# Moving 4 of 400 embedding gathers from GpSimd to single-row fetches that SyncE issues from registers

## The chip, the cores and the metric

The kernel runs on one core of one Trainium2 chip. The metric is the device time of one execution in microseconds. The kernel before ran 17 times: median 1652.48 us, from 1648.65 to 1654.3 us.

## The reference

The inputs are 1024 sequences of 50 item numbers, a length for each, a table of 100001 embedding rows of 128 floats, and a scale and a shift. Cut to what matters:

```python
emb = emb_table.at[0].set(0.0)
e = emb[seq]                                   # 1024 x 50 x 128
prefix = jnp.cumsum(e, axis=1)
denom = jnp.minimum(t_idx[None, :], lengths[:, None])
uF = prefix / denom[:, :, None]
mean, var = uF.mean(axis=0), uF.var(axis=0)    # over the 1024 sequences
y = (uF - mean) * lax.rsqrt(var + BN_EPS) * gamma + beta
def step(v, x):                                # 50 steps, one after the other
    v = v + (x - v) / TAU
    spike = atan_spike(v - V_TH)               # 1 where v >= 1
    v = v - spike * V_TH
    return v, spike
_, spikes = lax.scan(step, v0, x_seq)
scores = spikes.mean(axis=0) @ emb.T           # 1024 x 100001
```

## The kernel before

There are two stages. The first computes, for 1024 sequences and 128 features, how many of the 50 steps spiked. The second multiplies these counts with the whole table and writes 409.6 MB of scores.

The order of the instructions on each engine is the order in which the code is written (a manual schedule); waits between engines are semaphores that the framework adds.

In the first stage a step `t` goes like this. `gather(t)` (defined at L183) asks GpSimd for eight indirect DMAs (L187), one for each block of 128 sequences: each fetches 128 table rows of 512 bytes into one 128x128 piece of the tile `e`. The tile pool `gather` has two such tiles, so the gather of step t+1 may only begin when TensorE has read the tile of step t-1. At step t the kernel first issues `gather(t + 1)`, then TensorE transposes the eight pieces of `e` into the two PSUM banks `pre[0]` and `pre[1]`, where they add to the running sum (L296, four pieces for each bank, each matmul waiting for the landing of its own piece). VectorE then scales each bank and takes its statistics (L305, L306), TensorE adds the correction for the zero row of the next step (`correct`, L253), VectorE and ScalarE form mean, variance and the normalised input (L316 to L339), VectorE updates the membrane potential `v` (L348, L342), and TensorE adds the spikes to `sums` (`counted`, L264). Steps 42 and 44 also transpose one 1024-row part of the table each, for the second stage (`prepare`).

SyncE (SP) issues, in this order: the item numbers `idx` (1024 x 50, laid out 128 partitions x 8 blocks x 50 steps), the lengths, row 0 of the table, scale and shift, then six loads of 3 MB of the table (`fetch`, L97) for the second stage, and after that nothing until the first store of scores (L158) at the stage's end. DMAs from SP use eight completion semaphores in turn, and a DMA waits until the one eight places before it has landed.

The second stage turns the table (`prepare`: L119, L141, L142), multiplies it (L149), evicts with VectorE and ScalarE (L454, L456) and stores from SP (L158).

Of the kernel before, what the change touches and what calls it, by code (L numbers as in the profile page):

```python
# [12 lines left out]
F32 = mybir.dt.float32  # L13
# [7 lines left out]
P = 128  # L21
# [4 lines left out]
BANK = 512  # L26
# [8 lines left out]
def rec_kernel(  # L35
# [9 lines left out]
    nc = tc.nc  # L45
    B, T = seq.shape
    N, D = table.shape
    NB = B // P
# [24 lines left out]
    rows = {}  # L73
# [9 lines left out]
    def group(g):  # L83
        at = g if g < AHEAD else AHEAD - 2 + g % 2
        r = rowp.tile([P, GROUP, HALF], F32, tag=f"rows{at}", name=f"rows_{g}")
        for k in range(GROUP):
            rows[g * GROUP + k] = r[:, k, :]
        return r

    def fetch(r, q, n):  # L90

        engine = nc.sync if q < AHEAD * GROUP else nc.scalar
        k = q % GROUP
        n = min(n, parts - q)
        whole = n - (size(q + n - 1) < HALF)
        if whole:
            engine.dma_start(  # L97
                out=r[:, k : k + whole, :],
                in_=table[q * HALF : (q + whole) * HALF, :].rearrange("(q p k) d -> p q (k d)", p=P, k=KQ),
            )  # L100
        if whole < n:
            full, rest = divmod(size(parts - 1), P)
            c1 = (parts - 1) * HALF
            r = r[:, k + whole, :].rearrange("p (k d) -> p k d", d=D)
            if full:
                engine.dma_start(
                    out=r[:, :full, :],
                    in_=table[c1 : c1 + full * P, :].rearrange("(k p) d -> p k d", p=P),
                )
            if rest:  # L110
                engine.dma_start(out=r[:rest, full, :], in_=table[c1 + full * P : N, :])
# [21 lines left out]
    def prepare(q, pt):  # L133
        turned(q, pt)
        split[q] = hi, lo = free.pop(0)
        hw = size(q)
        if hw % 2:
            nc.vector.memset(hi[:, hw : hw + 1].bitcast(F32), 0.0)
            nc.vector.memset(lo[:, hw : hw + 1].bitcast(F32), 0.0)
        vp, vh, vl = views(q, pt, hi, lo)  # L140
        nc.scalar.copy(vh, vp)  # L141
        nc.vector.tensor_tensor(vl, vp, vh.bitcast(F32), ALU.subtract)  # L142
# [18 lines left out]
    with ExitStack() as ph:  # L161
        once = ph.enter_context(tc.tile_pool(name="once", bufs=1))
# [7 lines left out]
        idx = once.tile([P, NB, T], I32, tag="idx", name="idx")  # L170
# [8 lines left out]
        for g in range(AHEAD):  # L179
            fetch(group(g), g * GROUP, GROUP)  # L180

        es = {}

        def gather(t):
            es[t] = gp.tile([P, B], F32, tag="e", name=f"e_{t}")
            for n in range(NB):
                nc.gpsimd.indirect_dma_start(  # L187
                    out=es[t][:, n * P : (n + 1) * P],
                    out_offset=None,
                    in_=table,  # L190
                    in_offset=bass.IndirectOffsetOnAxis(ap=idx[:, n, t : t + 1].bitcast(U32), axis=0),
                )

        make_identity(nc, ident)
        gather(0)


# [47 lines left out]
        def only(t):  # L245

            l = sp.tile([P, D], F32R, tag="l", name=f"l_{t}")
            nc.scalar.activation(l, r0n, AF.Copy, scale=sel[:, t : t + 1])
            return l

        def correct(t, l):
            for h in range(B // BANK):
                nc.tensor.matmul(  # L253
                    pre[h],
                    lhsT=l,
                    rhs=zT[:, h * BANK : (h + 1) * BANK],
                    start=t == 0,
                    stop=False,
                    skip_group_check=True,
                )  # L260

        def counted(t, s):
            for h in range(B // BANK):
                nc.tensor.matmul(  # L264
                    sums[h],
                    lhsT=ident_h,
                    rhs=s[:, h * BANK : (h + 1) * BANK],
                    start=t == 0,
                    stop=t == T - 2,
                    skip_group_check=True,  # L270
                )
# [11 lines left out]
        for t in range(T):  # L283
            last = t == T - 1
            if t + 1 < T:
                gather(t + 1)
            e = es.pop(t)
            if last:
                s = lp.tile([P, B], BF16, tag="s", name=f"s_{t - 1}")
                nc.vector.tensor_single_scalar(s, v, V_TH, ALU.is_ge)  # L290
                nc.vector.tensor_tensor(negv, s, v, ALU.subtract)
            uF = up.tile([P, B], F32, tag="uF", name=f"uF_{t}")
            bs = sp.tile([P, B // BANK, 6], F32, tag="bs", name=f"bs_{t}")
            for h, cs in enumerate(halves):
                for k in range(0, BANK, P):
                    nc.tensor.matmul(  # L296
                        pre[h][:, k : k + P],
                        lhsT=e[:, h * BANK + k : h * BANK + k + P],
                        rhs=ident,
                        start=False,  # L300
                        stop=last,
                        is_transpose=True,
                        skip_group_check=True,
                    )
                nc.vector.scalar_tensor_tensor(uF[:, cs], rlen[:, cs], 1.0 / (t + 1), pre[h], ALU.max, ALU.mult)  # L305
                nc.vector.bn_stats(bs[:, h, :], uF[:, cs])  # L306
            if not last:
                correct(t + 1, l)
            else:

                counted(t - 1, s)
                count = once.tile([P, B], F32, tag="zT", name="count")
                for h, cs in enumerate(halves):
                    nc.scalar.copy(count[:, cs], sums[h])
            mv = sp.tile([P, 2], F32, tag="mv", name=f"mv_{t}")
            nc.vector.bn_aggr(mv, bs.rearrange("p h s -> p (h s)"))  # L316


            r = sp.tile([P, 1], F32, tag="r", name=f"r_{t}")
            nc.scalar.activation(r, mv[:, 1:2], AF.Sqrt, bias=eps)  # L320
            nc.scalar.activation(uF, uF, AF.Identity, bias=mv[:, 0:1], scale=-1.0)


            if t and not last:
                s = lp.tile([P, B], BF16, tag="s", name=f"s_{t - 1}")
                nc.vector.tensor_single_scalar(s, v, V_TH, ALU.is_ge)  # L326
                counted(t - 1, s)

            nc.vector.reciprocal(r, r)
            q = sp.tile([P, 1], F32, tag="q", name=f"q_{t}")  # L330
            nc.vector.tensor_mul(q, r, r)
            nc.vector.scalar_tensor_tensor(q, mv[:, 1:2], BN_EPS, q, ALU.add, ALU.mult)  # L332
            nc.vector.tensor_scalar(q, q, -0.5, 1.5, ALU.mult, ALU.add)
            a = sp.tile([P, 1], F32, tag="a", name=f"a_{t}")
            nc.vector.tensor_scalar(a, q, r, hgb[:, 0:1], ALU.mult, ALU.mult)  # L335


            def x(vt, cs):
                nc.scalar.activation(vt, uF[:, cs], AF.Identity, bias=hgb[:, 1:2], scale=a)  # L339

            def step(vt, cs):
                nc.vector.scalar_tensor_tensor(vt, negv[:, cs], -0.5, vt, ALU.mult, ALU.add)  # L342

            if not last:
                vt = vp.tile([P, B], F32, tag=f"v{t % 2}", name=f"v_{t}")
                x(vt, whole)
                if t:
                    nc.vector.tensor_tensor(negv, s, v, ALU.subtract)  # L348
                step(vt, whole)
                v = vt  # L350
                if t + 2 < T:
                    l = only(t + 2)

                if t in (T - 8, T - 6):
                    q = (t - T + 8) // 2
                    prepare(q, vp.tile([P, HALF], F32, tag="v1", name=f"pt_{q}"))
# [53 lines left out]
    for c, W in enumerate(WIDTHS):  # L410
# [30 lines left out]
        for n in range(NB):  # L441
            if c == 0 and n == 0:
                continue
            pool, tag, most = turns[blocks % len(turns)]
# [51 lines left out]
```

## Time and profile before

| what | value |
|---|---|
| median of 17 runs | 1652.48 us (1648.65 to 1654.3) |
| the profiled execution, its own time | 1653.87 us |
| its span in the profile | 1652.1 us |
| first store of scores issued | 587.68 us after the span's start |
| GpSimd busy | 379.2 us, 23% of the span, nearly all of it in the first stage |
| VectorE busy | 939.9 us, 57% |
| TensorE busy | 1112.6 us, 67% |
| mean granted TensorE clock | 0.802 |

The profile page gives, for one execution, the busy time of each engine, the span in 40 slices, the DMA queues, the chain of work that ended last, and groups of equal instructions with busy time, mean duration and the idle time before them. The trace behind it gives the instructions in order of time (the timeline: start, duration, engine, line, operation, tile written<-tiles read, and in brackets the idle time before and what ended it), the waits of an engine, and the busy time of chosen stretches. "SPq" is an instruction that SP executes to issue a DMA; its duration is that of the issue, not of the transfer. "Remote" stands where the profile couldn't name what ended a wait.

In 40 slices of 41.3 us, GpSimd's busy share (tenths), the DMA share and the moved GB/s show the two stages; the first ends in the fifteenth slice:

```
POOL 6666666666666500000000000000000000000000
DMA  9511111111111169999999999999999999999998
GB/s 340 214 44 48 48 43 48 48 48 43 47 48 46 39 280 409 417 422 397 426 429 427 426 429 430 418 425 428 420 428 409 413 428 425 414 427 410 396 422 359
```

### The profile page before, as it was taken

How to read it: one execution, taken by the hardware profiler on the slowest of the kernel's cores; microseconds unless marked ns; L12 is line 12 of the kernel's file. 1: busy time of each engine (PE TensorE's matmuls, PEld its weight loads, DVE VectorE, ACT ScalarE, POOL GpSimd, SP SyncE). 2: the span in 40 equal slices, each digit the busy share in tenths (PEclk: the TensorE clock that was granted, in tenths of full speed). 3: DMA queues.
4: the chain of work that ended last, by engine and by line, in shares of the span. 5: the costliest groups of instructions: out<-in, count | busy, mean ns of one | idle time of the engine just before them, and what ended most of it. 6: DMA issues, size and time to landing. Idle time of an engine off the chain costs nothing.

```text
span 1652.1 us, 12555 instructions
## 1 busy us (share of the span) xinstructions
PE 1112.6 (67%) x4538; PEld 828.6 (50%) x4548; DVE 939.9 (57%) x1161; ACT 630.6 (38%) x700; POOL 379.2 (23%) x406
## 2 busy tenths in 40 slices
PE   4333334433443488889987888878888888788785
PEld 2122212211222266667766666666666666666664
DVE  4566656655665666557655455545455555555553
ACT  2222222222222255545544444444444444444442
POOL 6666666666666500000000000000000000000000
PEclk7555555555555589999999999999999999999998
DMA  9511111111111169999999999999999999999998
GB/s 340 214 44 48 48 43 48 48 48 43 47 48 46 39 280 409 417 422 397 426 429 427 426 429 430 418 425 428 420 428 409 413 428 425 414 427 410 396 422 359
DMA packets 53691, 488.14 MB, mean 295 GB/s; under 512 B 11995, under 2 KB 12796, under 8 KB 32380
## 3 DMA queue, kind: packets, MB, share of 16 engines
q1 hardware_dynamic: 31984, 428.77, 61.7%
q0 software_dynamic: 12800, 26.24, 6.1%
q10 hardware_dynamic: 8844, 32.33, 5.0%
q8 instruction: 36, 0.59, 0.1%
q14 instruction: 27, 0.22, 0.0%
HBM read 77.69 MB, written 409.60 MB: 295 GB/s over the span
## 4 chain that ended last, share of the span: by engine, by line
DMA 48%; DVE 21%; PE 10%; another core or an unknown queue 9%; ACT 6%; issue 5%; POOL 1%; DVEq 0%; ACTq 0%; SPq 0%
DMA scores<-o 47%; PE po L149 9%; ACT o L456 4%; DVE bs L306 4%; DVE uF L305 4%; DVE v L342 3%; DVE s L326 3%; DVE negv L348 2%; DVE o L454 2%; ACT v L339 1%; POOL e L187 1%; DVE a L335 1%; DVE mv L316 1%; DVE q L332 0%
## 5 line engine op out<-in xcount | busy, mean ns | idle before, releaser
L454 DVE TENSOR_SCALAR o<-po 128x1024 f32<-128x1024 f32 x391 | 463.7, 1221 | 353.0 <-DMA scores<-o 322.2
L456 ACT ACTIVATE o<-po 128x1024 f32<-128x1024 f32 (+1 forms) x391 | 388.1, 1019 | 550.2 <-DMA scores<-o 346.0
L187 POOL DMA_INDIRECT e<-in_L_rec_emb_table,idx x400 | 378.5, 946 | 187.3 <-issue 114.6
L149 PE MATMUL po<-pairs,countB 128*128 128x512 f32 x1168 | 314.7, 416 | 66.7 <-ACT o L456 49.5
L149 PEld LDWEIGHTS po<-pairs,countB 128*128 128x128 f32 x1168 | 225.9, 198 | 131.4 <-ACT o L456 64.3
L149 PE MATMUL po<-pairs,countC 128*128 128x512 f32 x876 | 238.6, 418 | 44.7 <-ACT o L456 44.7
L253 PE MATMUL pre<-zT,l 128*128 128x512 f32 x100 | 74.1, 743 | 254.6 <-DVE uF L305 188.3
L149 PEld LDWEIGHTS po<-pairs,countC 128*128 128x128 f32 x876 | 169.3, 200 | 91.0 <-ACT o L456 56.2
L253 PEld LDWEIGHTS pre<-zT,l 128*128 128x128 f32 x100 | 27.5, 277 | 294.1 <-issue 201.4
L305 DVE SCALAR_TENSOR_TENSOR uF<-rlen,pre 128x512 f32<-128x512 f32 x100 | 67.9, 679 | 175.1 <-remote 115.7
L320 ACT ACTIVATE r<-mv,eps 128x1 f32<-128x1 f32 x50 | 14.7, 295 | 373.1 <-DVE mv L316 259.2
L142 DVE TENSOR_TENSOR pairs<-pt,pairs 128x1024 fp32r<-128x1024 f32 (+1 forms) x73 | 88.4, 1217 | 96.4 <-ACT pairs L141 96.2
L296 PE MATMUL pre<-ident,e 128*128 128x128 f32 x400 | 105.4, 423 | 25.2 <-DMA e<-in_L_rec_emb_table,idx 19.0
L119 PE MATMUL pt<-ident,rows 128*128 128x128 f32 x782 | 111.3, 289 | 8.2 <-ACT o L456 3.6
L119 PEld LDWEIGHTS pt<-ident,rows 128*128 128x128 f32 x782 | 100.8, 152 | 28.6 <-issue 10.0
L296 PEld LDWEIGHTS pre<-ident,e 128*128 128x128 f32 x400 | 85.3, 223 | 58.6 <-DMA e<-in_L_rec_emb_table,idx 33.2
L149 PE MATMUL po<-hi,countB 128*128 128x512 f32 x200 | 83.5, 417 | 18.5 <-ACT o L456 14.1
L264 PE MATMUL sums<-s,ident_h 128*128 128x512 bf16 x88 | 44.9, 601 | 64.5 <-issue 34.3
L149 PE MATMUL po<-lo,countB 128*128 128x512 f32 x200 | 81.1, 405 | 0.0
L149 PE MATMUL po<-pairs,countA 128*128 128x512 f32 (+1 forms) x292 | 73.6, 394 | 10.2 <-ACT o L456 10.1
L141 ACT CAST pairs<-pt 128x1024 fp32r<-128x1024 f32 (+1 forms) x73 | 73.6, 1008 | 14.8 <-PE pt L119 14.5
L149 PE MATMUL po<-hi,countC 128*128 128x512 f32 x150 | 62.8, 419 | 16.2 <-ACT o L456 16.1
(76 smaller groups left out, 849.7 us busy)
## 6 DMA issues: line engine op xcount, KB each, us to landing
scores<-o SPq DMA_DIRECT2D x96, 3072.0 KB, 20.6
scores<-o SPq DMA_DIRECT2D x32, 1536.0 KB, 9.0
rows<-in_L_rec_emb_table ACTq DMA_DIRECT2D x20, 1536.0 KB, 30.1
scores<-o SPq DMA_DIRECT2D x22, 1024.0 KB, 8.6
rows<-in_L_rec_emb_table SPq DMA_DIRECT2D x6, 3072.0 KB, 42.7
scores<-o SPq DMA_DIRECT2D x8, 2048.0 KB, 13.2
scores<-o SPq DMA_DIRECT2D x8, 1872.5 KB, 11.3
e<-in_L_rec_emb_table,idx POOLq DMA_INDIRECT x400
```

Of the source, the lines that this page charges most:

```text
L119: nc.tensor.transpose(pt[:, k0 : k0 + kw], r[:kw, k0 : k0 + D], ident[:kw, :kw])
L141: nc.scalar.copy(vh, vp)
L142: nc.vector.tensor_tensor(vl, vp, vh.bitcast(F32), ALU.subtract)
L149: nc.tensor.matmul(po[:, :kw], lhsT=counts[n], rhs=part[:, k0 : k0 + kw], start=j == 0, stop=j == 1,)
L187: nc.gpsimd.indirect_dma_start(out=es[t][:, n * P : (n + 1) * P], out_offset=None, in_=table, in_offset=bass.IndirectOffsetOnAxis(ap=idx[: ...
L253: nc.tensor.matmul(pre[h], lhsT=l, rhs=zT[:, h * BANK : (h + 1) * BANK], start=t == 0, stop=False, skip_group_check=True,)
L296: nc.tensor.matmul(pre[h][:, k : k + P], lhsT=e[:, h * BANK + k : h * BANK + k + P], rhs=ident, start=False, stop=last, is_transpose=True, ...
L305: nc.vector.scalar_tensor_tensor(uF[:, cs], rlen[:, cs], 1.0 / (t + 1), pre[h], ALU.max, ALU.mult)
L306: nc.vector.bn_stats(bs[:, h, :], uF[:, cs])
L326: nc.vector.tensor_single_scalar(s, v, V_TH, ALU.is_ge)
L454: nc.vector.tensor_scalar_mul(o[:, h0 : h0 + hw], po[:, :hw], 1.0 / T)
L456: nc.scalar.mul(o[:, h0 : h0 + hw], po[:, :hw], 1.0 / T)
```

## The change

For the first block of 128 sequences, at the steps 44, 45, 46 and 47, GpSimd no longer gathers. In its place SP, after its six loads of the table, goes through the 128 partitions: it reads four item numbers of one partition from `idx` into registers (one instruction), and for each of the four computes the row's address in registers (one instruction for two multiplications) and issues a DMA of this one 512-byte row into a tile `aside_44` to `aside_47`. These tiles have memory of their own and are written once. That makes 128 register loads, 512 register computations and 512 DMAs on SP, all between its sixth load of the table and its first store. GpSimd issues 396 gathers, seven at each of the four steps. TensorE's first transpose of each of these steps reads `aside` in place of the first piece of `e`, and waits for the semaphores of these row fetches.

The built order shows the following besides: the fetched rows take their turn among SP's eight completion semaphores, so the eighth row fetch waits until the sixth load of the table has landed, and each later one until the row fetch eight places before has landed. The rows are fetched partition by partition, with the four steps inside, so the last row of `aside_44` is the 509th of the 512. On the other engines the order of the work is as before.

```diff
         for g in range(AHEAD):
             fetch(group(g), g * GROUP, GROUP)
 
+        aside = {}
+        for t0, many in ((T - 6, 4),):
+            for t in range(t0, t0 + many):
+                aside[t] = once.tile([P, P], F32, tag=f"aside{t}", name=f"aside_{t}")
+            for p in range(P):
+                _, items = nc.values_load_multi_w_load_instructions(
+                    idx[p : p + 1, 0, t0 : t0 + many],
+                    engines=[mybir.EngineType.SP],
+                    min_val=0,
+                    max_val=N - 1,
+                    skip_runtime_bounds_check_because="items are rows of the table; the transfer checks its own bounds",
+                )
+                for j, item in enumerate(items):
+                    nc.sync.dma_start(out=aside[t0 + j][p : p + 1, :], in_=table[bass.ds(item, 1), :])
+
         es = {}
 
         def gather(t):
             es[t] = gp.tile([P, B], F32, tag="e", name=f"e_{t}")
-            for n in range(NB):
+            for n in range(t in aside, NB):
                 nc.gpsimd.indirect_dma_start(
...
                     nc.tensor.matmul(
                         pre[h][:, k : k + P],
-                        lhsT=e[:, h * BANK + k : h * BANK + k + P],
+                        lhsT=aside[t] if h == k == 0 and t in aside else e[:, h * BANK + k : h * BANK + k + P],
                         rhs=ident,
```

## The prediction

> **What bounds the kernel now.** I read the chain of waits first, to see which stage pays for what.
>
> ```profile
> DMA scores<-o 47%; PE po L149 9%; ACT o L456 4%; DVE bs L306 4%; DVE uF L305 4%; DVE v L342 3%; DVE s L326 3%; DVE negv L348 2%; DVE o L454 2%; ACT v L339 1%; POOL e L187 1%; DVE a L335 1%; DVE mv L316 1%; DVE q L332 0%
> ```
>
> Nearly half of the chain is stores of scores, from the first at 587.68 us on. That stage is as long as its stores and isn't touched: what ends the first stage d us earlier ends the kernel d us earlier. So only the first 588 us matter. There the chain names VectorE, but the groups and GpSimd's own waits tell who paces it:
>
> ```profile
> L187 POOL DMA_INDIRECT e<-in_L_rec_emb_table,idx x400 | 378.5, 946 | 187.3 <-issue 114.6
> ```
> ```profile
> POOL e L187 <- issue: 114.6, 376, 0.3
> POOL e L187 <- remote: 63.8, 15, 5.6
> ```
>
> A gather is busy for 0.946 us and 376 of the 400 start 0.30 us after the one before: 1.25 us each, 400 x 1.25 = 500 us of the stage. The 15 waits ended by "remote" are all the slack that GpSimd has, 63.8 us. The timeline shows one, and the stage's end:
>
> ```profile
> 475.25 0.95 POOL L187 DMA_INDIRECT e<-in_L_rec_emb_table,idx  x1 [0.31 <-issue]
> 480.48 0.95 POOL L187 DMA_INDIRECT e<-in_L_rec_emb_table,idx  x1 [4.28 <-remote]
> 481.73 0.95 POOL L187 DMA_INDIRECT e<-in_L_rec_emb_table,idx  x1 [0.30 <-issue]
> ```
> ```profile
> 566.21 0.95 POOL L187 DMA_INDIRECT e<-in_L_rec_emb_table,idx  x1 [0.31 <-issue]
> 568.52 0.69 DVE L305 SCALAR_TENSOR_TENSOR uF<-rlen,pre 128x512 f32<-128x512 f32 x1 [9.54 <-remote]
> ...
> 571.40 0.69 DVE L305 SCALAR_TENSOR_TENSOR uF<-rlen,pre 128x512 f32<-128x512 f32 x1 [1.47 <-remote]
> ```
>
> Two things are to be seen. GpSimd restarts after such waits at 310.43, 344.43, 378.42, 412.44, 446.49, 480.48: every 34.0 us, 24 gathers (three steps, 30.0 us) and 4.0 us of idling for a free tile. And VectorE runs two steps 7.49 us apart (L305 at 543.91 and 551.40), then waits, and is released 5.2 us after the last gather that GpSimd could issue (566.21 to 571.40; likewise 475.25 to 480.24). Why TensorE's transposes come out so late in every third step the trace doesn't say; that their end is tied to GpSimd's last gather it does. So the stage goes at GpSimd's pace: a gather less is 1.25 us less, and VectorE has room, since its step of 7.49 us is under the 10.0 us of eight gathers or the 8.75 us of seven.
>
> **What is removed.** 4 gathers x 1.25 us = 5.0 us. They fall behind the waits of the stage, not into them, if the pattern of waits stays: step 44's missing gather releases the wait that ends at 514.75 by 1.25 us, those of 45 and 46 the one at 537.45 by 3.75 us in all, that of 47 brings the last gather from 566.21 to 561.2 us. Four transposes read another tile: the same instruction and form. Each waits for two semaphores more than before, one extra wait on TensorE, at most the 0.3 us between two of its rows here, and in steps where its data are long there: 0 taken, up to 1.2 us in the range.
>
> **What is added.** SP was idle then:
>
> ```profile
> SPq L158 <- ACT o L390: 552.2, 3, 550.5
> ```
>
> 550.5 us of waiting between the last load and the first store hide the new work as long as it ends in time. When can it start, and when must it end? The eighth row waits for the sixth load of the table:
>
> ```profile
> 40.00:60.00 20.00, 5.61 (x13) 3.28 (x15) 10.04 (x19) 2.96 (x5) 11.06 (x13) 0.50 1.03 393
> 60.00:80.00 20.00, 7.26 (x22) 4.39 (x21) 11.28 (x22) 5.63 (x8) 14.91 (x16) 0.50 0.25 69
> ```
>
> The last column is GB/s. From 80 to 100 us it is 43; the 26 above that are 0.52 MB, at 393 GB/s 1.3 us: the loads end at about 61.3 us. The first use is step 44's first transpose:
>
> ```profile
> 521.33 1.91 PE L296 MATMUL pre<-ident,e 128*128 128x128 f32 x8
> ```
>
> 521.33, less the 1.25 us gained by then: 520.1. All but 3 of the rows must have landed, so SP has 458.8 us, 0.896 us for a row or 3.58 us for a group of four. A row costs an issue, a register computation, and a quarter of a register load. Issues of other transfers:
>
> ```profile
> 2.82 0.43 SPq L177 DMA_DIRECT2D gb<-in_L_rec_gamma  x1
> 3.29 0.43 SPq L178 DMA_DIRECT2D gb<-in_L_rec_beta  x1
> 3.77 33.35 SPq L97 DMA_DIRECT2D rows<-in_L_rec_emb_table  x6
> ```
> ```profile
> 1507.25 0.35 ACTq L97 DMA_DIRECT2D rows<-in_L_rec_emb_table  x1
> 1507.63 1.28 ACTq L106 DMA_DIRECT2D rows<-in_L_rec_emb_table  x1
> 1508.94 1.72 ACTq L111 DMA_DIRECT2D rows<-in_L_rec_emb_table  x1
> ```
>
> The smallest transfers on SP (0.5 KB, like a row) follow each other by 0.47 us. The dearest issue that isn't a load of megabytes is L111, 33 partitions of 512 bytes: 1.72 us. It stands directly behind another slow one, and it is ACT's; a row has the bytes of `gb` and SP's queue. I take 0.47 and keep 1.72 as the upper end. A computation in registers has no row; the gaps between SP's issues are 0.04 to 0.05 us: 0.05 taken, 0 to 0.3 (the gap on GpSimd) possible. A load from SBUF into a register has none either: from 0 up to 3.0 us, the time in which the smallest timed DMA (`len_i`, 4 KB) goes out and lands, which is a longer way. I take 1.0 us, an estimate nearer the lower end because no DMA is in it. A group: 4 x (0.47 + 0.05) + 1.0 = 3.08 us; 128 of them 394 us; done at 455 us, 65 us before they are needed: 0 on the path. From both sides: 4 x 0.47 = 1.88 us a group, done at 302 us; or 4 x (1.72 + 0.3) + 3.0 = 11.1 us, done at 1480 us, 960 us late.
>
> The waits between row fetches cost nothing at that pace: eight rows back is 6.2 us ago, twice the landing of `len_i`. On the DMA engines the rows are 0.26 MB beside the 47 GB/s that this stretch moves: 0, or bounded in the rivals by what a delayed gather does. SP's stores come after, 130 us later: 0.
>
> The Trainium skill ("DMA: Bandwidth & Descriptors", section "Latency and other measured facts") puts the floor of a register load from a tensor at about 600 ns. By it a group would be 2.68 us and the rows done at 404 us; no row here shows one. The same page (section "Why a DMA increments its semaphore by 16 and not by 1") speaks against the change: a transfer whose shape doesn't split over 16 engines makes the issuing sequencer write the rest of the count itself. L111's 33 partitions, at 1.72 us, agree with that; if every row were such a one, a group would be 4 x 1.77 + 1.0 = 8.08 us and the rows done at 1096 us. The page gives no price for these writes.
>
> **The sum** against the profiled execution: 1653.87 - 5.0 = 1648.9; that one lies 1.39 us over the median, so 1647.5 us by the median.
>
> **The rivals.**
> - *SP is late (slower).* A row needs more than 0.896 us, which is where a load costs over 1.50 us at an issue of 0.47. TensorE waits at step 44, GpSimd stops two tiles on, and every us late is one on the end, since the steps and gathers behind it still have to be done. With a load of 2.0 us a group is 4.08 us, done at 583.5, 63.4 us late: 1647.5 + 63.4 = 1711 us. It is slower than before from 0.906 us a row. For it: L106 and L111, and that nothing here shows a load. Against: the issues at 0.47.
> - *More of the three-step waits (slower).* The rows' transfers and semaphore counts share the DMA engines with the gathers. Where a wait came after two steps instead of three (from 218.96 to 242.46) 2 steps took 23.5 us, 11.75 a step against 11.33. If that were so for the 35 steps from 62 to 455 us: 35 x 0.42 = +14.6, -5.0: 1662 us. Against: the DMA share is 0.18 there.
> - *One wait less (faster by more).* At step 48 TensorE starts its transposes at 556.31, and the last piece, issued at 556.20, makes it wait until 558.85. After the change TensorE comes 3.75 us earlier and that gather 5.0, so this wait is gone, and with it perhaps the one of VectorE up to 571.40. Then VectorE's second half of step 48 is at 552.72 - 3.75 + 7.49 = 556.5 in place of 571.4, and the last step, whose pieces land by about 564, no longer waits: -14.9, 1637.6 us. Against: step 45 shows such a wait where TensorE had not waited for a piece.
> - *Nothing.* The 5.0 us go into GpSimd's idling, a wait that something else ends: 1652.5 us. Against: the releases follow the last gather.
>
> **How the numbers follow.** The forecast has 0.44, SP late 0.22, more waits 0.08, one wait less 0.15, nothing 0.11. 0.2% is 3.3 us, about what runs of this kernel can tell from no change. The forecast is faster but for 0.03 that belong to "same": faster 0.41 + 0.15 = 0.56, same 0.11 + 0.03 = 0.14, slower 0.30. The time is the forecast's, 1647.5; its own range is 1645 to 1650. The range for 8 in 10 goes down to 1636 for the missing wait, up past 1662 to 1668, which takes in rows late by up to 20 us (0.04 of the 0.22): 0.18 left out above.
>
> **What would show it.** Right: 396 gathers 1.25 us apart, the last at about 561 us, the first store at 582.7; SP's row fetches ended before 520 us; TensorE's transposes of `aside` waiting for nothing. Each price is then read off: the spacing of row fetches within a group and between groups. Wrong: TensorE idle until a row fetch lands; more than 15 waits of GpSimd by "remote", or fewer; SP's first store held up by rows still going out.

## The result and the profile after

The changed kernel takes 1779.97 us (median of 9 runs, 1774.19 to 1785.16), the one before 1652.76 us in the runs beside it: ratio 1.0771 [1.0760, 1.0781], slower by 127 us. The profiled execution took 1787.07 us, with a span of 1785.3 us against 1652.1 before, 133.2 us more. All lines below the added code have moved by 17: the gathers are L204 now, the row fetches L197, the transposes L313, `uF` L322.

The chain of waits shows a line that was not there before, and the stores' share fell only because the whole grew:

```profile
DMA scores<-o 43%; PE po L149 8%; SPq L197 4%; ACT o L473 4%; SPq L189 2%; DVE o L471 2%; DVE bs L323 0%; DVE uF L322 0%; DVE v L359 0%; ACT pairs L141 0%; DVE s L343 0%; PE pt L119 0%; DVE pairs L142 0%; DVE negv L365 0%
```

SP's row fetches (L197) and the register loads before them (L189) stand on the path now. The groups of the page and GpSimd's own waits (engine, tile and line, what it waited for: us in total, times, the longest) say who paid:

```profile
L204 POOL DMA_INDIRECT e<-in_L_rec_emb_table,idx x396 | 374.7, 946 | 330.7 <-PE pre L313 140.6
L313 PE MATMUL pre<-ident,aside 128*128 128x128 f32 x4 | 1.7, 427 | 136.9 <-DMA aside<-in_L_rec_emb_table 136.7
```
```profile
POOL e L204 <- PE pre L313: 140.6, 3, 137.3
POOL e L204 <- issue: 111.3, 365, 0.3
POOL e L204 <- remote: 61.7, 20, 4.7
POOL e L204 <- PE pre L270: 13.4, 4, 3.5
```

Four gathers are gone at 0.946 us each, with no change in the price of the others. Against that stand two single waits: TensorE's first transpose of `aside` waits 136.7 us, and GpSimd, two tiles ahead, 137.3 us for that transpose. The timelines of TensorE and of GpSimd show them:

```profile
525.63 1.01 PE L281 MATMUL sums<-s,ident_h 128*128 128x512 bf16 x2 [1.26 <-DVE s L343]
663.36 0.45 PE L313 MATMUL pre<-ident,aside 128*128 128x128 f32 x1 [136.71 <-DMA aside<-in_L_rec_emb_table]
```
```profile
527.35 0.94 POOL L204 DMA_INDIRECT e<-in_L_rec_emb_table,idx  x1 [0.30 <-issue]
665.57 0.94 POOL L204 DMA_INDIRECT e<-in_L_rec_emb_table,idx  x1 [137.28 <-PE pre L313]
```

Step 44's transposes begin at 663.36 in place of 521.33, 142.0 us late. The first store follows 58.0 us behind them and not 66.4, since the pieces of steps 44 and 45 were there already. So it goes out at 721.37 in place of 587.68, 133.7 us late; the span grew by 133.2. All of the loss is this one wait.

SP's own timeline, cut at three windows (start, us, how many row fetches they cover):

```profile
61.98 457.90 SPq L197 DMA_DIRECT2D aside<-in_L_rec_emb_table  x264
```
```profile
539.82 120.20 SPq L197 DMA_DIRECT2D aside<-in_L_rec_emb_table  x207
```
```profile
721.37 3.62 SPq L158 DMA_DIRECT2D scores<-o  x4
```

From 62 to 520 us, while GpSimd gathers, a row takes 457.90 / 264 = 1.73 us. From 540 us on, with GpSimd and TensorE stopped for want of these rows, the same instructions take 120.20 / 207 = 0.58 us a row. The instructions of L197 by kind (in ns the shortest, the median and the longest, then the first and the last start) tell what became longer:

```profile
L197 SPq FUSED_REGOPS  x512: 2/37/1419, 37.7 to 663.2; - x171
L197 SPq MOVE aside<-in_L_rec_emb_table x512: 2/29/1398, 37.8 to 663.3; - x171
L197 SPq DMA_DIRECT2D aside<-in_L_rec_emb_table x512: 2/225/7557, 38.1 to 663.3; - x171
```

Not only the DMAs: a computation in registers, 0.037 us in the median, and a move of a register, 0.029 us, last up to 1.4 us. (The one DMA of 7.56 us is set aside here: the run with quick rows below, `f1_after`, has such a one too, 8.36 us.) What stretches such an instruction is the question of the experiments.

### The profile page after: what moved, and what is told of

Same layout as the page of the kernel before. It is cut to its first block, busy times and chain, and to the rows that moved or that the text cites. A ratio compares the mean times of both kernels' runs of the same rounds, so it can differ in the third digit from the quotient of the medians.

```text
span 1785.3 us, 14221 instructions
## 1 busy us (share of the span) xinstructions
PE 1109.4 (62%) x4538; PEld 832.3 (47%) x4548; DVE 940.5 (53%) x1161; ACT 630.9 (35%) x700; POOL 375.4 (21%) x402
## 4 chain that ended last, share of the span: by engine, by line
DMA 43%; PE 8%; SPq 6%; ACT 5%; DVE 4%; issue 4%; another core or an unknown queue 0%; DVEq 0%; ACTq 0%
DMA scores<-o 43%; PE po L149 8%; SPq L197 4%; ACT o L473 4%; SPq L189 2%; DVE o L471 2%; DVE bs L323 0%; DVE uF L322 0%; DVE v L359 0%; ACT pairs L141 0%; DVE s L343 0%; PE pt L119 0%; DVE pairs L142 0%; DVE negv L365 0%
## 5 line engine op out<-in xcount | busy, mean ns | idle before, releaser
L204 POOL DMA_INDIRECT e<-in_L_rec_emb_table,idx x396 | 374.7, 946 | 330.7 <-PE pre L313 140.6
L270 PE MATMUL pre<-zT,l 128*128 128x512 f32 x100 | 75.8, 760 | 270.4 <-DVE uF L322 216.9
L322 DVE SCALAR_TENSOR_TENSOR uF<-rlen,pre 128x512 f32<-128x512 f32 x100 | 68.1, 681 | 316.6 <-remote 161.2
L270 PEld LDWEIGHTS pre<-zT,l 128*128 128x128 f32 x100 | 28.1, 282 | 311.7 <-issue 197.3
L313 PE MATMUL pre<-ident,e 128*128 128x128 f32 x396 | 98.5, 420 | 11.9 <-DMA e<-in_L_rec_emb_table,idx 5.6
L313 PEld LDWEIGHTS pre<-ident,e 128*128 128x128 f32 x396 | 85.2, 226 | 36.2 <-issue 27.4
L313 PE MATMUL pre<-ident,aside 128*128 128x128 f32 x4 | 1.7, 427 | 136.9 <-DMA aside<-in_L_rec_emb_table 136.7
```

What stands on the lines that cost most here:

```text
L204: nc.gpsimd.indirect_dma_start(out=es[t][:, n * P : (n + 1) * P], out_offset=None, in_=table, in_offset=bass.IndirectOffsetOnAxis(ap=idx[: ...
L270: nc.tensor.matmul(pre[h], lhsT=l, rhs=zT[:, h * BANK : (h + 1) * BANK], start=t == 0, stop=False, skip_group_check=True,)
L313: nc.tensor.matmul(pre[h][:, k : k + P], lhsT=aside[t] if h == k == 0 and t in aside else e[:, h * BANK + k : h * BANK + k + P], rhs=ident ...
```

## The experiments

The runs fell on chips of two kinds. On kind A the kernel before takes 1652.2 to 1653.8 us, as in the result; on kind B 1576.2 to 1577.0 us. Each run is compared with the kernel before on its own chip. The stores' stage is alike on both: from the first store to the end of the span 1652.1 - 587.68 = 1064.4 us on A, 1063.0 on B (`b4_bufs3`, below: 1574.2 - 511.24). It is the first stage that differs: on B its steps follow each other by 10.0 us, eight gathers, without the waits after every third step.

### What stretches the row fetches

Four theories: the cost lies in the instructions themselves (register load, computed addresses); in the one-row transfers; in GpSimd's gathers, whose traffic or whose making slows SP; or in whatever else runs then. The first four runs fell on a chip of kind B.

`e1_static` takes the registers away and fetches fixed rows, so at the four steps the first block's rows are others than the reference's:

```diff
-                _, items = nc.values_load_multi_w_load_instructions(idx[p : p + 1, 0, t0 : t0 + many], ...)
-                for j, item in enumerate(items):
-                    nc.sync.dma_start(out=aside[t0 + j][p : p + 1, :], in_=table[bass.ds(item, 1), :])
+                for j in range(many):
+                    item = (p * many + j) * 97
+                    nc.sync.dma_start(out=aside[t0 + j][p : p + 1, :], in_=table[item : item + 1, :])
```

> The same 512 one-row fetches from SP, but from fixed rows of the table, so that no item number is loaded and no address computed (the rows of the steps 44 to 47 are others than the reference's). Theory 'gathers': while GpSimd gathers, each of SP's instructions takes about 0.7 us, whatever it is; a row of the changed kernel is 3.25 instructions (a quarter of a load, a computation, a move, the DMA) and took 1.7 us. One instruction a row then makes about 0.7 us, the rows are done at 62 + 512 x 0.7 = 420 us, before step 44, and the time is 1647 to 1653 us. Rival 'one-row transfer': the issue of a transfer of one row is what costs 1.7 us; rows done past 650 us, 1780 us.

Measured: 1571.38 against 1576.53 us, ratio 0.9968 [0.9956, 0.9979]. The rows went out at 0.30 us each and were done at 214 us. With the rows in time, the change is worth 5.15 us, which is close to the forecast's 4 x 1.25 = 5.0. What was expected above was worked out for the chip of the result.

`e2_one` lets GpSimd make one gather a step in place of eight, and all transposes but those of `aside` read this piece, so seven eighths of the embeddings are left out:

```diff
-            for n in range(t in aside, NB):
+            for n in (1,):
...
-                        lhsT=aside[t] if h == k == 0 and t in aside else e[:, h * BANK + k : h * BANK + k + P],
+                        lhsT=aside[t] if h == k == 0 and t in aside else e[:, P : 2 * P],
```

> The changed kernel with one gather a step in place of eight (seven); all transposes but that of the fetched rows read this one piece (seven eighths of the embeddings are left out). TensorE, VectorE and ScalarE work as before. Theory 'gathers': with GpSimd idle for most of a step SP's row costs 0.57 to 0.7 us as it does after 540 us in the changed kernel, rows done at 355 to 420 us; steps 7.5 us apart, first stage some 400 to 470 us, time 1470 to 1540 us. Rival 'other engines': SP is slowed by what TensorE, VectorE and ScalarE do in the steps, and was quick after 540 us because they stood still too: a row still costs 1.4 us or more, rows done past 780 us, time over 1840 us.

`e3_ahead` puts 200 additional gathers into one spare tile ahead of the first step; `e4_plain` replaces each gather by ScalarE's plain load of 128 consecutive rows, the same bytes, so the look-up is left out except in the rows that SP fetches:

```diff
+        spare = once.tile([P, P], F32, tag="spare", name="spare")
+        for k in range(200):
+            nc.gpsimd.indirect_dma_start(out=spare, out_offset=None, in_=table, in_offset=...)
         gather(0)
```

> The changed kernel with 200 more gathers, into a tile that nobody reads, before the first: for some 250 us GpSimd gathers and TensorE, VectorE and ScalarE have nothing to do. Theory 'gathers': SP's rows cost 1.4 to 2.2 us in this stretch (some 90 to 140 rows from 62 to 255 us). Rival 'other engines': 0.57 us, some 330 rows. The time itself is about 250 us longer less what SP gains by it.

```diff
             for n in range(t in aside, NB):
-                nc.gpsimd.indirect_dma_start(out=es[t][:, n * P : (n + 1) * P], ...)
+                at = (t * NB + n) * P
+                nc.scalar.dma_start(out=es[t][:, n * P : (n + 1) * P], in_=table[at : at + P, :])
```

> The changed kernel with each gather replaced by a plain load of 128 consecutive table rows, of the same 64 KB, issued by ScalarE (the items' embeddings are left out but for the fetched rows). Theory 'gathers', in the form that GpSimd's writing of descriptors is what slows SP: rows cost 0.57 to 0.7 us, done at 355 to 420 us, SP never late, time 1480 to 1650 us. In the form that the gathers' traffic on the DMA engines slows SP: rows cost over 1.2 us, done past 670 us, time over 1720 us.

Measured on kind B: `e2_one` 1465.34 us, rows at 0.58 us from 33 to 348 us; `e3_ahead` 2151.68 us, rows at 0.58 us, but the additional gathers waited for each other, 388.7 us in 198 waits, so GpSimd was never gathering back to back; `e4_plain` 1568.23 us, rows done at 450 us, 0.66 us each from 300 us on (228 in 150 us). There SP waited 93.4 us in 55 waits until one of the heavier plain loads had landed, and the stage waited 89.8 us for the rows, which neither theory had. On this chip no register computation of SP took over 0.051 us in these three runs. The four runs couldn't tell the theories apart, and showed that the chip had to be looked at.

### The chip

`a1_after` is the changed kernel unaltered and `a2_static` the kernel of `e1_static`, both on a chip of kind A.

> The changed kernel once more, unaltered, beside the kernel before on the same chip. The four runs above fell on a chip where the kernel before takes 1576.5 us and GpSimd never waits for a free tile. Theory 'gathers, where sequencers are slowed': where the kernel before takes about 1652 us, a row costs 1.4 to 2.2 us while GpSimd gathers and the time is 1775 to 1790 us; where it takes 1576 us a row costs 0.57 to 0.62 us, the rows are done at 355 to 390 us, before step 44, and the time is 5 us under that of before, 1571.5 us. Rival 'register work': what made SP slow was the loading and computing of addresses, which the first experiment left out; then the changed kernel is late by over 100 us on either chip.

> The fetches from fixed rows again (other rows than the reference's at the steps 44 to 47), beside the changed kernel of this call. Where the kernel before takes 1576 us: 1571.4 us as before. Where it takes 1652 us: theory 'gathers' has 0.7 to 0.9 us a row, done at 420 to 520 us, and 1645 to 1665 us; rival 'one-row transfer' has 1.7 us a row and 1780 us.

Measured: `a1_after` 1781.12 against 1652.23 us, 1.0787 [1.0768, 1.0806], its rows from 38 to 655 us, TensorE's wait 129.6 us: the result again. `a2_static`, one execution: 1653.21 us. Its rows took 0.61 us each (470 of them in 288.28 us), less than the 0.7 to 0.9 expected but twice their price on kind B, and were done at 368.5 us, 150 us before their use. One instruction for a row is quick enough there, 3.25 (a load for four, a computation, a move, a DMA) are not. But with the rows in time the change still brought nothing in this execution on kind A. GpSimd's waits of `a2_static`, beside those that the prediction showed of the kernel before:

```profile
POOL e L198 <- issue: 112.2, 368, 0.3
POOL e L198 <- remote: 57.5, 17, 5.8
POOL e L198 <- PE pre L264: 17.7, 5, 4.4
```

Waits for a free tile come to 57.5 + 17.7 = 75.2 us, before to 63.8 + 4.1 = 67.9 us. The last gather starts at 566.05 us, before at 566.21. GpSimd idled 7.3 us more, and of the gathers' 5.0 us nothing was left.

Then the changed kernel on a third chip of kind B and twice more on kind A:

> The changed kernel, unaltered, once more in search of a chip where the kernel before takes 1576 us. There, theory 'gathers, where sequencers are slowed': rows of 0.57 to 0.62 us, done at 355 to 390 us, 5.0 us less than before, about 1571.3 us; rival 'register work': late. Where the kernel before takes 1652 us: 1781 us again.

> The changed kernel, unaltered. On a chip where the kernel before takes 1576 us: theory 'gathers, where sequencers are slowed' has rows of 0.57 to 0.62 us, done at 355 to 390 us, and 5.0 us less than before, 1571.2 us, as the fetches from fixed rows had; rival 'register work' has it late. Where it takes 1652 us: 1781 us again.

> The changed kernel, unaltered. Where the kernel before takes 1576 us: theory 'gathers, where sequencers are slowed' has rows of 0.57 to 0.62 us, done at 355 to 390 us, and 5.0 us less than before, about 1571.3 us; rival 'register work' has it late. Where it takes 1652 us: 1781 us again.

Measured: `c1_after` 1782.51 against 1653.08 us, 1.0791 [1.0768, 1.0815]; `d1_after` 1779.19 against 1653.84 us, 1.0749 [1.0707, 1.0790]; `f1_after`, on kind B, 1572.51 against 1577.04 us, 0.9970 [0.9959, 0.9982]: 4.5 us faster, where 5.0 were forecast. SP's instructions by kind in `f1_after`, the register loads (L189) first, then GpSimd's waits:

```profile
L189 SPq TENSOR_LOAD <-idx x128: 463/564/717, 37.2 to 355.1; - x128
L197 SPq FUSED_REGOPS  x512: 37/37/51, 37.7 to 357.0; - x171
L197 SPq MOVE aside<-in_L_rec_emb_table x512: 29/29/29, 37.8 to 357.1; - x171
L197 SPq DMA_DIRECT2D aside<-in_L_rec_emb_table x512: 224/225/8363, 37.9 to 357.1; - x171
```
```profile
POOL e L204 <- issue: 115.6, 379, 0.3
POOL e L204 <- DMA e<-in_L_rec_emb_table,idx: 3.0, 10, 0.3
POOL e L204 <- DMA idx<-in_r_seq: 2.6, 1, 2.6
POOL e L204 <- PE pre L313: 1.8, 6, 0.3
```

The computation takes 0.037 to 0.051 us throughout, though GpSimd gathers without a pause; the rows end at 357 us; and there is no wait by "remote" at all. So one and the same kernel is 4.5 us faster on one kind of chip and 125 to 129 us slower on the other.

### GpSimd alone

`b1_one` is `e2_one` again, on another chip of kind B:

> One gather a step in place of eight (seven eighths of the embeddings are left out), again, for the case that the chip is one where the kernel before takes 1652 us. There, theory 'gathers': SP's rows at 0.57 to 0.75 us, done before 450 us; rival 'other engines': over 1.4 us a row though GpSimd mostly stands still, done past 700 us. Where the kernel before takes 1576 us: 1465 us as before.

Measured: 1466.5 us, rows as before, 33 to 348 us. Nothing new.

`b2_ahead` mends `e3_ahead` with six spare tiles, so that GpSimd gathers back to back for 250 us while TensorE, VectorE and ScalarE have nothing to do; `c2_ahead` is the same on a chip of kind A:

```diff
+        spare = [once.tile([P, P], F32, tag=f"spare{k}", name=f"spare_{k}") for k in range(6)]
+        for k in range(200):
+            nc.gpsimd.indirect_dma_start(out=spare[k % 6], out_offset=None, in_=table, in_offset=...)
         gather(0)
```

> The changed kernel with 200 more gathers, into six tiles that nobody reads, before the first: GpSimd gathers without a pause for some 250 us while TensorE, VectorE and ScalarE have nothing to do. Where the kernel before takes 1652 us: theory 'gathers' has SP's rows at 1.4 to 2.8 us from 62 to 255 us (70 to 140 rows), rival 'other engines' 0.57 us (330 rows). Where it takes 1576 us: 0.57 to 0.62 us under either.

> 200 more gathers ahead of the first, into six tiles that nobody reads: some 250 us in which GpSimd gathers without a pause and TensorE, VectorE and ScalarE have nothing to do. Where the kernel before takes 1652 us: theory 'gathers' has SP's rows at 1.4 to 2.8 us from 62 to 255 us (70 to 140 rows), rival 'other engines' 0.57 us (330 rows). Where it takes 1576 us: 0.58 us, as before.

Measured: 1820.73 us on B and 2031.87 us on A. The windows' table for 100 to 200 us (the length, then the busy time of PE, PEld, DVE, ACT and POOL with the number of instructions, the clock, the DMA share and GB/s), and SP's row fetches in the same stretch, first on B (timeline), then on A (all of SP's instructions by kind):

```profile
100.00:200.00 100.00, 0.00 (x0) 0.00 (x0) 0.00 (x0) 0.00 (x0) 75.48 (x80) 1.00 0.20 54
```
```profile
100.19 99.36 SPq L197 DMA_DIRECT2D aside<-in_L_rec_emb_table  x172
```
```profile
100.00:200.00 100.00, 0.00 (x0) 0.00 (x0) 0.00 (x0) 0.00 (x0) 75.47 (x80) 1.00 0.20 53
```
```profile
L197 SPq DMA_DIRECT2D aside<-in_L_rec_emb_table x23: 700/709/709, 99.5 to 198.9; - x23
L197 SPq FUSED_REGOPS  x22: 700/705/709, 100.9 to 196.1; - x22
L197 SPq MOVE aside<-in_L_rec_emb_table x22: 700/704/709, 102.3 to 197.5; - x22
L189 SPq TENSOR_LOAD <-idx x5: 700/700/709, 109.3 to 182.1; - x5
```

The load is the same on both, with 80 gathers, a DMA share of 0.20 and TensorE, VectorE and ScalarE idle. Yet SP issues 172 rows on B, 0.58 us each, and 23 on A. There 22 rows go by from 99.5 to 198.9 us, 4.52 us each; 1.4 to 2.8 were expected.

The lines of A show more than a slowness. Whatever SP does, a move, a register computation, a load or a DMA, lasts 0.700 to 0.709 us, and each of the 138 instructions that SP starts from 62 to 255 us starts 1.400 us after the one before. So an instruction isn't stretched in proportion to its work: from each start to its end, and from that end to the next start, 0.70 us pass, and a row costs 3.25 x 1.40 = 4.55 us. In the changed kernel itself, where the gathers have pauses, SP is held for a part of the time only: its median computation there is still 0.037 us.

What sets this pace no run shows. One thing happens at every start and at every end in all the runs: the profiler marks the time. Every execution on record has a span that was taken so, and none without is there to compare. A rival therefore stays untested: the taking of the marks may itself hold SP up while GpSimd gathers on such a chip. Whether SP would be late without the profiler is open with it.

Later in `c2_ahead` GpSimd stands still, waiting 99.78 us for a free tile, while the same rows still go out:

```profile
825.07 75.12 SPq L197 DMA_DIRECT2D aside<-in_L_rec_emb_table  x129
```

Here it is 0.58 us a row again. No work of TensorE, VectorE or ScalarE is needed for the slowness.

`d2_plain` asks whether it is the gathers' traffic or their making: the kernel of `e4_plain` on kind A.

> Each gather replaced by a plain load of 128 consecutive rows, the same 64 KB, issued by ScalarE (the items' embeddings are left out but for the fetched rows). Where the kernel before takes 1652 us: if the gathers' way of making descriptors is what slows SP, rows cost 0.57 to 0.8 us as they did where it takes 1576 us, and the time is about 1568 us; if their traffic on the DMA engines does, rows cost over 1.2 us and the time is over 1700 us. Where it takes 1576 us: 1568 us as before.

Measured: 1567.66 us, where `e4_plain` had 1568.23 on kind B. SP's instructions of `d2_plain`:

```profile
L197 SPq FUSED_REGOPS  x512: 37/37/51, 59.4 to 450.1; - x171
L197 SPq MOVE aside<-in_L_rec_emb_table x512: 29/29/29, 59.5 to 450.2; - x171
L197 SPq DMA_DIRECT2D aside<-in_L_rec_emb_table x512: 224/225/328, 70.2 to 450.2; - x171
```

No computation is longer than 0.051 us, with 64 KB loaded in place of each gather (70 GB/s from 100 to 200 us against 45 with the gathers in the changed kernel). So it is not the bytes as such: the slowness goes with transfers that GpSimd makes. Whether it is the making, or the way in which these transfers are carried out, isn't separated. And with no gather in the kernel the two kinds of chip take the same time, up to step 44 as well: TensorE's wait for the rows begins at 360.9 us here and at 361.2 in `e4_plain`.

### What the saved gathers are worth

`b3_two` moves one gather each of steps 48 and 49 in place of 44 to 47; `b4_bufs3` is the kernel before with three tiles in the pool `gather`. Both on kind B:

```diff
-        for t0, many in ((T - 6, 4),):
+        for t0, many in ((T - 2, 2),):
```

> The change at two steps, 48 and 49, in place of four: 256 rows, 64 of them... two a partition, so that SP is done in time even at 1.75 us a row (62 + 448 = 510 us; step 48 is at 556 us). Theory 'late': with nothing late the change does what its two gathers are worth, 2.5 us less than before. Rival 'traffic': SP's rows slow the gathers or TensorE by themselves; then no gain or a loss, where rows are slow.

```diff
-        gp = ph.enter_context(tc.tile_pool(name="gather", bufs=2))
+        gp = ph.enter_context(tc.tile_pool(name="gather", bufs=3))
```

> The kernel before with three tiles for the gathers in place of two. Theory 'slowed until GpSimd runs dry': where the kernel before takes 1652 us, its late transposes end only when GpSimd has no tile left; with a third tile GpSimd goes on for a step more, the late step is 10 us longer, and a cycle is four steps with 4.0 us of idling, 44.0 us: 11.0 us a step in place of 11.33, some 16 us less, about 1636 us. Rival 'fixed length': the late step lasts some 12.5 us whatever GpSimd does; then GpSimd no longer runs dry, a step is 10.0 us, and the time is about 1590 us. Where the kernel before takes 1576 us: no change.

Measured: `b3_two` 1575.96 against 1576.17 us, 0.9997 [0.9988, 1.0006]; `b4_bufs3` 1576.25, 1.0001 [0.9992, 1.0011]. A third tile does nothing where GpSimd never waits. Of the two late gathers, VectorE's lines show where the gain went; `b3_two` first, then `b4_bufs3`:

```profile
494.36 0.69 DVE L322 SCALAR_TENSOR_TENSOR uF<-rlen,pre 128x512 f32<-128x512 f32 x1 [1.06 <-PE pre L313]
...
503.06 0.68 DVE L322 SCALAR_TENSOR_TENSOR uF<-rlen,pre 128x512 f32<-128x512 f32 x1
```
```profile
495.43 0.69 DVE L305 SCALAR_TENSOR_TENSOR uF<-rlen,pre 128x512 f32<-128x512 f32 x1 [2.38 <-PE pre L296]
...
504.13 0.68 DVE L305 SCALAR_TENSOR_TENSOR uF<-rlen,pre 128x512 f32<-128x512 f32 x1
```

Step 48 comes 1.07 us earlier, that is its own gather. Step 49 follows 8.7 us behind it in both without having waited: the last step is VectorE's, and its gather is hidden. So of 2.5 us expected 1.0 is left, too little to be measured.

`d3_bufs3` is `b4_bufs3` on kind A: do three tiles remove the wait after every third step?

> The kernel before with three tiles for the gathers in place of two. Where the kernel before takes 1652 us: theory 'slowed until GpSimd runs dry': the late transposes end only when GpSimd has no tile left; with a third tile the late step is 10 us longer, a cycle is four steps and 44.0 us, 11.0 us a step in place of 11.33: some 16 us less, about 1636 us. Rival 'fixed length': a late step lasts 12.5 us whatever GpSimd does; GpSimd no longer runs dry, a step is 10.0 us, about 1590 us. Where it takes 1576 us: no change, as before.

Measured: 1655.2 against 1653.84 us, 1.0013 [1.0003, 1.0023]. Both numbers were missed. GpSimd's and VectorE's timelines of `d3_bufs3` round one such wait:

```profile
294.22 0.94 POOL L187 DMA_INDIRECT e<-in_L_rec_emb_table,idx  x1 [0.30 <-issue]
299.60 0.94 POOL L187 DMA_INDIRECT e<-in_L_rec_emb_table,idx  x1 [4.44 <-remote]
```
```profile
294.39 0.69 DVE L305 SCALAR_TENSOR_TENSOR uF<-rlen,pre 128x512 f32<-128x512 f32 x1 [7.88 <-remote]
...
299.36 0.69 DVE L305 SCALAR_TENSOR_TENSOR uF<-rlen,pre 128x512 f32<-128x512 f32 x1 [3.55 <-remote]
```

TensorE's eight transposes for these two stand at 283.86 to 285.77 in the trace. VectorE gets the second bank 13.6 us later, 5.1 us after GpSimd's last gather (294.22) and just before it restarts. With one tile more GpSimd is further ahead, and still runs dry every 34.1 us (restarts at 231.41, 265.52, 299.60, 333.73). So the release does follow GpSimd's pause, as the prediction read it, but lack of tiles is not what brings the late step about. What does was not found.

## Why the prediction was wrong, point by point

**Who paces the stage, and what a gather is worth: right on kind B.** 5.0 us were forecast; 4.5 (`f1_after`) and 5.15 (`e1_static`) were measured there. On kind A, with the rows in time, it was nothing (`a2_static`, one execution): the rival *nothing*, to which 0.11 was given, with its 1652.5 us. "They fall behind the waits of the stage, not into them, if the pattern of waits stays" is the condition that failed: idling rose by 7.3 us.

**What an issue costs: the step that failed.** "The smallest transfers on SP (0.5 KB, like a row) follow each other by 0.47 us." These rows start at 2.82 and 3.29 us; GpSimd's first gather is at 4.26. The other rows taken, ScalarE's at 1507 us, come 940 us after its last. Every price of an issue came from a stretch without gathers and was put into one that is full of them. That is how the sum came to "0 on the path" for SP; measured were 142.0 us at step 44. As prices for SP alone they were too dear: on kind B a group of four rows takes 4 x 286.50 / 492 = 2.33 us (the 492 rows from 64 to 350 us) where 3.08 were taken, and the rows were done at 357 us, not 455. An issue is 0.225 us, not 0.47; there are moves of 0.029 us which the sum did not have. On kind A a row takes 1.73 us beside the gathers, a group 6.9 us. The upper end of the sum, 11.1 us a group, held it; the value taken lay near the lower end, and the range of the time allowed for only 20 us of lateness.

**The Trainium skill's two figures.** For the floor of a register load, some 600 ns ("DMA: Bandwidth & Descriptors", section "Latency and other measured facts"), `f1_after` has a row: a load of four item numbers takes 0.564 us in the median, from 0.463 to 0.717. The rest of the 2.33 us fits: 4 x (0.037 + 0.029 + 0.225) = 1.16 are the other twelve instructions, which leaves 0.61 for the thirteen gaps, 0.05 each. So the page's figure was near, and nearer than the 1.0 taken, though loads fall below it. The rule on the sequencer that writes the rest of the count itself (section "Why a DMA increments its semaphore by 16 and not by 1") shows no price here: the whole issue of a one-row DMA is 0.225 us, and whether the rule applied to it no run shows. What was missed stands in neither.

**The rival that came true: SP is late.** Its place, its point (0.896 us a row) and its price, a us on the end for each us late, held: 142.0 us at step 44, 133.7 at the first store, less by the 8.3 us by which GpSimd was ahead. Its cause did not: a load of 2.0 us was imagined, 63 us late; the load kept a median of 0.560 us in the result's profile, and what failed is that every instruction of SP is held to one pace for part of the time, a move like a load. That is also why the number of instructions decides: 1 for a row is in time on kind A at 0.61 us, 3.25 are not.

**The waits between row fetches and the DMA engines: right beside gathers.** On kind B no row fetch waited for one before it (`f1_after`); in the result such waits came to 5.2 us in 7. Beside the plain loads it would not have held: in `d2_plain` row fetches waited 93.5 us in 50 waits for plain loads to land, though none of SP's register computations became longer. **More three-step waits:** on kind A the waits by "remote" rose from 15 to 20 in the profile of the result and took 61.7 us against 63.8. But with those that L270's matmuls ended (13.4 us against 4.1), waits for a free tile came to 75.1 us against 67.9, 7.2 more, as in `a2_static` (72.9 to 78.0 us in the four profiles of the changed kernel on kind A). That is half of this rival's 14.6 us; what it cost can't be told beside the 142 us. **One wait less:** not seen.

What stays open: why GpSimd's gathers hold SP's instructions to one pace on some chips and not on others, and whether they would without the profiler's marks; whether the late releases of TensorE's transposes there are the same thing, which their absence on kind B and the gap of 13.6 us in `d3_bufs3` suggest, but no run shows; and whether registers loaded for more rows at once would be in time on kind A, which wasn't tried. No kernel with the whole computation in it was faster than the kernel before on kind A.

## What to carry to other kernels

Price an instruction from a stretch in which the other engines do what they will do where it is to run; if no such row exists, that cost is unknown, however many quiet rows agree. Count every instruction of a queue, registers and moves too, not the transfers alone: if each is held to a fixed pace, their number decides. When an instruction is slow, read the times of unlike instructions beside it: equal times point at a pace from outside, not at the work. And run a change of a few us on more than one chip before believing its sign.

## What the runs showed of the hardware

- On some chips SP's instructions are held to one pace while GpSimd gathers without a pause: a start every 1.400 us in `c2_ahead`, 0.70 us for a register computation in place of 0.037, with TensorE, VectorE and ScalarE idle. On other chips, with 80 gathers in the same 100 us, they are not (`b2_ahead`, a register computation at most 0.051 us). With plain loads from ScalarE's queue it was not seen on either (at most 0.051 us in `e4_plain` and `d2_plain`). Whether it would be so without the profiler is not shown.
- The same program takes 1576 to 1577 us on three chips and 1652 to 1654 us on others, nearly 5% more; without gathers (`e4_plain`, `d2_plain`, one execution each) the difference is 0.6 us.
- On kind B a row fetched by a constant address cost SP 0.30 us (`e1_static`), by a register 0.58 us (`f1_after`), with the transfer's issue 0.225 to 0.25 us in both. A load into registers took 0.564 us for four item numbers (`f1_after`) and 0.747 us for two (`b3_two`), in the median.
- The granted clock did not tell these chips apart: from 100 to 200 us it was 1.00 in `f1_after` and 0.50 in `b3_two`, both with steps 10.0 us apart, and 0.56 in the kernel before on kind A.
